# A convolution network's last two tiles, worked by halves of the images

## The chip, the cores and the metric

The kernel runs on one core of a Trainium2 chip, in one launch. A core has five engines that run beside each other: TensorE (PE, matmuls; its weight loads are listed as PEld), VectorE (DVE), ScalarE (ACT), GpSimd (POOL) and SyncE (SP, which here only issues DMAs). Sixteen DMA engines move data between the on-chip memory and DRAM. The metric is the time of the program on the device in microseconds; less is better. The span of a profile runs from the first to the last instruction of the profiled execution.

## The reference

The input is 1024 images of 16 x 16 pixels and 16 channels, in f32. Four layers follow each other, each of them `x = x + layer(norm(x))`, where the norm is taken over groups of channels. Layers 0 and 2 are a tensor-train product and a 3 x 3 convolution. Layers 1 and 3 are of one kind, and layer 3 is the one that the change touches:

```python
xt = jnp.transpose(x, (0, 3, 2, 1))
pre = _alive(xt)
y1 = _depthwise(xt, conv1_w, conv1_b)          # 3 x 3, per channel
y2 = _depthwise(xt, conv2_w, conv2_b)
p = jnp.concatenate([xt, y1, y2], axis=1)
flat = p.reshape(B * W * Hh, 48)
h = jax.nn.relu(flat @ fc0_w.T + fc0_b)        # 48 -> 128
d = (h @ fc1_w.T + fc1_b).reshape(B, C, W, Hh) # 128 -> 16
xn = xt + d
post = _alive(d)
xn = xn * (pre & post)
```

`flat` is cut into rows of 48 across the channel axis of an image, so one row of `fc0` mixes neighbouring pixels and channels of one image. All images are worked alike, and none depends on another.

## The kernel before, in words

**Tiles.** The images are worked in two chunks of 512 (`NB`). A chunk lies on chip as 32 tiles of 128 partitions by 512 columns: a column is an image, a partition one of 128 values, a tile is numbered `8 * q + w2`, with `q` a quarter of the channels and `w2` a pair of image columns. Two buffers, `X0` and `X1`, hold one chunk each. At the end of the kernel `layer_nca(X1, 1, 3, L3, xo)` works layer 3 on the second chunk in `X1`, while `output_steps(0)` writes the first chunk's images, which already lie in DRAM as tiles: it loads them line by line (`xs`), transposes them on VectorE (L1005) and stores them (L1010).

**Quads.** The work of `layer_nca` is a list of 64 quads `(q, w2, v)`. A quad is four rows of `fc0`, one in each of TensorE's four row groups. Each row is a sum of three small products, `T.matmul(ph, w, x)` at L1495, with 32 input rows, 128 outputs and 512 columns; the weights `wq` come from DRAM per quad. ScalarE applies bias and ReLU on the way out of PSUM (`hid`, L1498). Then `fc1` (L1346) brings the four hidden rows down to the outputs `po`; two quads, `v = 0` and `v = 1`, fill one tile.

**Order.** `plan()` writes the order of TensorE's work in advance, as slots: a slot is either one product in each row group or an `fc1`. It keeps a simple model of ScalarE (`evacs`, in slots), of six PSUM banks for `ph` (`BANKS`), and starts a quad at most two ahead of the `fc1` that is due. Work that follows is not waited for at once: `after(n, fn)` puts it n slots later. Each engine runs its own instructions strictly in the order of the program.

**The end of a tile.** `finish` adds bias and input into `u` on VectorE (L1358), `residual` multiplies by the mask and adds to the residual `r` (L1397, L1398), on GpSimd for all tiles but the last, (3, 7), which VectorE does. `fetch` has loaded `r` from DRAM when the tile's first `fc1` was emitted. On the second chunk `turn` follows eight slots later: four transposes on TensorE, one per 128 images (`ptx`, L1407; the PSUM pool `o` with its two banks is shared with `po`), and two copies on VectorE (`evac`, L159) into `xo`. `xo` is the buffer `X0` seen as `[image % 128, image group g, line h, column w, channel c]`, so that an image's values lie next to each other.

**The stores.** When all 32 tiles have been turned, eight DMAs of 1 MB store `xo` (L1657), two halves of the lines by four image groups. They stand behind the whole layer in the program.

**How `output_steps` is spread.** `run` takes steps with a lower and an upper bound as shares of the layer's slots, and interleaves them.

Of the kernel before, what the change touches and what calls it, by code (L numbers as in the profile page):

```python
# [12 lines left out]
ALU = mybir.AluOpType  # L13
# [5 lines left out]
B, S, C = 1024, 16, 16  # L19
P = 128  # L20
# [83 lines left out]
def conv_preact_kernel(ctx: ExitStack, tc: tile.TileContext, a: dict, out: bass.AP):  # L104
# [1180 lines left out]
    def layer_nca(X, n, l, L, xo=None):  # L1285


        st = {}
        quads = [(q, w2, v) for q in range(4) for w2 in range(8) for v in range(2)]
        AHEAD, FAR = 2, 3  # L1290
        BANKS, SKEW = 6, (0, 1, 2, 1)

        def rows_of(q, w2, v):
            return [16 * (4 * q + j) + 2 * w2 + v for j in range(4)]

        def weights(m):

            if m >= len(quads):
                return
            q, w2, v = quads[m]  # L1300
            slot = triple(2 * w2 + v)[1]
            if q > 0:
                st["wq", m] = work([P, 3, HID], "wq", "wq")
                nc.sync.dma_start(
                    st["wq", m],
                    L["wy"][q - 1].rearrange("g v h s k -> (g v h) s k")[:, slot : slot + 3],
                )

        def lines(m):


            if m >= len(quads) or triple(2 * quads[m][1] + quads[m][2])[0] < 2:
                return
            nx = st["nx", m] = work([P, 2, NB], "nx", "nx")
            for r in rows_of(*quads[m]):
                tiles = row_tiles(r)
                g = tiles[0][0] % 4
                over = [t[0] % C for t in tiles if t[0] % 4 != g]
                c, n1 = over[0], len(over)
                nc.sync.dma_start(  # L1320
                    nx[32 * g : 32 * g + 32, 0:n1],
                    X[32 * (c % 4) : 32 * (c % 4) + 32, 8 * (c // 4) : 8 * (c // 4) + n1],
                )
# [12 lines left out]
            for m in range(FAR):  # L1336
                lines(m)

        def fc1(q, w2, v, hid):
            if v == 0:  # L1340
                st["po"] = bank([P, NB], "o", "po1")
                if q > 0:
                    fetch(8 * q + w2)
            po = st["po"]
            for j in range(4):
                T.matmul(  # L1346
                    po[32 * j : 32 * j + 32], nca["w1"][:, v], hid[j], start=v == 0, stop=v == 1
                )
            if v == 1:
                finish(q, w2, po)  # L1350

        def finish(q, w2, po):
            if q == 0:
                V.tensor_scalar(
                    st["f", w2][64:96], po[96:128], nca["b1"][96:128], ALIVE, ALU.add, ALU.is_gt
                )
            u = st["u", q, w2] = work([P, NB], "u", "u")
            V.scalar_tensor_tensor(u, po, nca["b1"], X[:, 8 * q + w2], ALU.add, ALU.add)  # L1358
            if q > 0:
                residual(q, w2)  # L1360
                return

            ws = range(w2 - 1 if w2 else 0, 8 if w2 == 7 else w2)

            def masked():
                for w in ws:
                    mask(w)
                    residual(0, w)

            for w in ws:  # L1370
                fetch(w)
            after(3, masked)
# [17 lines left out]
            V.tensor_scalar(m, cnt[0], 0.5, None, ALU.is_gt)  # L1390
            V.scalar_tensor_tensor(m, cnt[1], 0.5, m, ALU.is_gt, ALU.mult)  # L1391

        def residual(q, w2):
            u, r = st["u", q, w2], st["r", q, w2]

            by = V if (q, w2) == (3, 7) else G
            by.tensor_tensor(u, u, st["m"][:, w2], ALU.mult)  # L1397
            by.tensor_tensor(r, r, u, ALU.add)  # L1398
            if xo is None:
                after(7, lambda: nc.sync.dma_start(tile_cw(xf[l + 1][n], 8 * q + w2), r))  # L1400
            else:
                after(8, lambda: turn(q, w2, r))

        def turn(q, w2, r):
            pt = psum([P, 4, 4, 2, S], "ptx")
            for bg in range(4):
                T.transpose(  # L1407
                    pt[:, bg].rearrange("p c v h -> p (c v h)"), r[:, bg * P : bg * P + P], ident
                )
            for v in range(2):  # L1410

                evac(
                    xo[:, :, :, 2 * w2 + v, 4 * q : 4 * q + 4].rearrange("p g h c -> p g c h"),
                    pt[:, :, :, v],
                )

# [7 lines left out]
        def plan():  # L1426

            todo = [[] for _ in range(4)]
            for m, quad in enumerate(quads):
                for j, r in enumerate(rows_of(*quad)):  # L1430
                    todo[row_tiles(r)[0][0] % 4].append((m, j, row_tiles(r)))
            left, ready = [4] * len(quads), [0.0] * len(quads)
            now, evacs, free_at, t, begun, f = [None] * 4, 0.0, [], 0, 0, 0
            while f < len(quads):
                if left[f] == 0 and ready[f] <= t:
                    yield f
                    f, t = f + 1, t + 1
                    continue
                free_at = [b for b in free_at if b > t]
                out = []  # L1440
                for g in range(4):
                    if now[g] is None and todo[g] and begun >= SKEW[g] and todo[g][0][0] <= f + 2:
                        if len(free_at) + sum(x is not None for x in now) < BANKS:
                            now[g] = [*todo[g].pop(0), 0]
                    if now[g] is not None:
                        m, j, tiles, k = now[g]
                        out.append((m, j, k))
                        now[g][3] += 1
                        if k == len(tiles) - 1:
                            evacs = max(evacs, t + 1.15) + 0.75  # L1450
                            free_at.append(evacs)
                            left[m], ready[m], now[g] = left[m] - 1, max(ready[m], evacs), None
                yield out
                t, begun = t + 1, begun + 1

        def step(slot):
            def go():
                t = st["slot"]
                if isinstance(slot, int):
                    q, w2, v = quads[slot]  # L1460
                    fc1(q, w2, v, [st["hid", slot, j] for j in range(4)])
                else:
                    for x in slot:
                        tile_of_row(*x)
                due = [fn for n, fn in later if n <= t]
                later[:] = [x for x in later if x[0] > t]
                for fn in due:
                    fn()
                st["slot"] = t + 1

            return go

        def tile_of_row(m, j, k):
            q, w2, v = quads[m]
            r = rows_of(q, w2, v)[j]
            tiles = row_tiles(r)
            if k == 0:
                if st.setdefault("begun", -1) < m:
                    st["begun"] = m
                    weights(m + AHEAD)  # L1480
                    lines(m + FAR)
                    if v == 0 and q == 0:
                        flags(w2)
                st["ph", m, j] = bank([P, NB], "h", "ph")
            ph = st["ph", m, j]
            ch, pair, pat = tiles[k]
            g = tiles[0][0] % 4
            rg = slice(32 * g, 32 * g + 32)
            if ch < C:
                w = nca["xw"][rg, XPATS.index(pat)]  # L1490
            else:
                w = st["wq", m][rg, TRIPLES[triple(2 * w2 + v)[0]].index(pat)]

            x = X[rg, 8 * (ch % C // 4) + pair] if ch % 4 == g else st["nx", m][rg, pair]
            T.matmul(ph, w, x, start=k == 0, stop=k == len(tiles) - 1)  # L1495
            if k == len(tiles) - 1:
                h = st["hid", m, j] = work([P, NB], "hid", "hid")
                A.activation(h, ph, AF.Relu, bias=nca["bt"][:, r : r + 1])  # L1498

        def rest():  # L1500
# [148 lines left out]
    with ExitStack() as es:  # L1649
        stage(es, dict(nca_sb, xs=2, xo=2), nca_ps)  # L1650

        xo = X0.rearrange("p n b -> p (n b)").rearrange("p (g h w c) -> p g h w c", g=4, h=S, w=S)
        run(layer_nca(X1, 1, 3, L3, xo), 280, (), (output_steps(0), 0.0, 1.0))
        for h in range(0, S, 8):
            for g in range(4):
                b0 = NB + g * P
                nc.sync.dma_start(  # L1657
                    out[b0 : b0 + P, h : h + 8].rearrange("b h w c -> b (h w c)"),
                    xo[:, g, h : h + 8].rearrange("p h w c -> p (h w c)"),
                )  # L1660


# [25 lines left out]
```

## Time and profile before

| | |
|---|---|
| Time, median of 3 runs | 3043.16 us (3041.85 to 3044.43) |
| Time of the profiled execution | 3042.73 us |
| Its span | 3041.0 us |
| Busy: PE / PEld / DVE / ACT / POOL | 98% / 41% / 58% / 36% / 22% |
| Mean DMA rate over the span | 138 GB/s |
| Rate while the image stores run | 376 GB/s |

The page's busy shares are means over all four layers. The tables by window show the busy time of each engine in a stretch (times are counted from the start of the span), then the granted clock of TensorE as a share of full speed, the busy share of the DMA engines and what they moved. In the chain of waits and in the timeline a line gives start, duration, engine, source line, the operation with its output and inputs, shapes, and the number of instructions merged. `xn` is the program's name for the buffers `X0` and `X1`, so a store `out_dram<-xn` reads `xo`. A f32 matmul leaves two records, and its end in the profile is modelled: what counts is the distance between starts.

### The profile page before, as it was taken

The numbers are of one execution on the slowest core, as the hardware profiler recorded it, in microseconds if no ns is written. First come the engines' busy times: TensorE is split into PE (matmuls) and PEld (weight loads), VectorE is DVE, ScalarE is ACT, GpSimd is POOL, SyncE is SP. The second block draws the span as 40 slices with busy tenths as digits, with TensorE's granted clock in tenths as the row PEclk, the third lists the DMA queues.
The fourth block names the chain that finished last, engine by engine and source line by source line (L and its number), as shares of the span: only waits on it lengthen the run. The fifth ranks groups of instructions, "written<-read, shape, count | busy, mean of one in ns | idle before, by whom it ended". The sixth has DMA issues, their size and how long they took to land.

```text
span 3041.0 us, 36525 instructions
## 1 busy us (share of the span) xinstructions
PE 2971.9 (98%) x13690; PEld 1239.6 (41%) x13690; DVE 1761.4 (58%) x2340; ACT 1099.3 (36%) x1806; POOL 671.6 (22%) x729
## 2 busy tenths in 40 slices
PE   7999999999999999999999999999999999999996
PEld 5544334444444444444444433333333333333332
DVE  5354337555554555544555668756977766856432
ACT  4431441000000000000101156666667656666563
POOL 1124670200000000000000015434542224432331
PEclk8999999999999999999999999999999999999998
DMA  8543664533334333332222235436437866343555
GB/s 310 225 126 99 147 150 151 166 109 109 109 109 149 124 109 109 109 102 88 88 88 94 71 131 167 137 119 204 124 121 183 193 109 199 123 127 110 155 158 197
DMA packets 251520, 418.37 MB, mean 138 GB/s; under 512 B 34868, under 2 KB 105064, under 8 KB 248272
## 3 DMA queue, kind: packets, MB, share of 16 engines
q1 hardware_dynamic: 225776, 362.53, 36.6%
q0 software_dynamic: 25376, 53.38, 8.5%
q8 instruction: 108, 1.77, 0.2%
q14 instruction: 68, 0.56, 0.1%
q10 hardware_dynamic: 192, 0.13, 0.0%
HBM read 238.58 MB, written 165.53 MB: 133 GB/s over the span
## 4 chain that ended last, share of the span: by engine, by line
PE 88%; issue 4%; POOL 2%; DVE 2%; DMA 2%; ACT 1%; SPq 0%; POOLq 0%; DVEq 0%; ACTq 0%
PE po L1134 51%; PE ph L1495 20%; PE po L1346 7%; PE pw L1057 3%; PE po L1222 2%; POOL xf L1271 1%; PE L_conv_pe L392 1%; PE ptin L866 1%; DVE bn L860 1%; POOL res L1398 1%; PE ptx L1407 1%; POOL u L1397 1%; PE po L1231 0%; ACT hx L1210 0%; DMA gq<-g_dram 0%
## 5 line engine op out<-in xcount | busy, mean ns | idle before, releaser
L1134 PE MATMUL po<-xn,w 128*128 128x512 f32 x3584 | 1575.6, 596 | 0.8 <-DVE xn L946 0.8
L1134 PEld LDWEIGHTS po<-xn,w 128*128 128x128 f32 x3584 | 670.8, 190 | 839.8 <-issue 820.9
L1498 ACT ACTIVATE hid<-ph,pack 128x512 f32<-128x512 f32 x1024 | 652.7, 686 | 381.5 <-PE ph L1495 271.6
L1170 DVE TENSOR_TENSOR r<-r,po 128x512 f32<-128x512 f32 x576 | 377.9, 684 | 577.5 <-PE po L1134 525.0
L1397 POOL TENSOR_TENSOR u<-u,mask 128x512 f32<-128x512 f32 x124 | 193.9, 1564 | 1820.9 <-DVE mask L1391 1404.2
L1062 ACT COPY w<-pw 128x512 f32<-128x512 f32 (+1 forms) x320 | 150.6, 557 | 1212.1 <-issue 1006.4
L1495 PE MATMUL ph<-xn,wq 32*128 32x512 f32 x3664 | 567.1, 611 | 0.0
L1495 PEld LDWEIGHTS ph<-xn,wq 32*128 32x128 f32 x3664 | 233.3, 184 | 270.0 <-issue 237.6
L1495 PE MATMUL ph<-xn,pack 32*128 32x512 f32 x1288 | 298.8, 625 | 4.9 <-ACT hid L1498 3.0
L1346 PE MATMUL po<-hid,pack 128*32 128x512 f32 x2048 | 281.7, 607 | 0.0
L1075 DVE TENSOR_TENSOR w<-w 128x512 f32<-128x512 f32 x320 | 210.9, 686 | 90.6 <-ACT w L1062 90.6
L655 DVE TENSOR_TENSOR xn<-xn,m 128x1024 f32<-128x1024 f32 x160 | 216.2, 1382 | 45.0 <-ACT m L678 44.8
L1358 DVE SCALAR_TENSOR_TENSOR u<-po,pack,xn 128x512 f32<-128x512 f32 x128 | 95.8, 749 | 203.3 <-PE po L1346 197.0
L1398 POOL TENSOR_TENSOR res<-res,u 128x512 f32<-128x512 f32 x124 | 206.5, 1666 | 9.7
L1222 PE MATMUL po<-xn,convw 128*128 128x512 f32 x368 | 166.2, 604 | 2.9 <-ACT conv L1270 2.9
L1495 PEld LDWEIGHTS ph<-xn,pack 32*128 32x128 f32 x1288 | 115.0, 185 | 104.3 <-issue 63.9
L1170 DVE TENSOR_TENSOR xn<-xn,po 128x512 f32<-128x512 f32 x96 | 64.4, 684 | 123.7 <-PE po L1134 123.3
L1346 PEld LDWEIGHTS po<-hid,pack 128*32 128x32 f32 x2048 | 42.8, 108 | 195.2 <-issue 144.3
L622 DVE TENSOR_TENSOR sq<-sq 128x1024 f32<-128x1024 f32 x78 | 109.8, 1407 | 13.3 <-ACT sq L640 12.6
L1222 PEld LDWEIGHTS po<-xn,convw 128*128 128x128 f32 x368 | 68.7, 191 | 99.7 <-issue 90.4
L404 POOL DMA_DIRECT2D L_conv_wy<-xn x160 | 88.8, 563 | 26.8 <-ACT xn L398 15.6
L1057 PE MATMUL pw<-R,gq 32*128 32x256 f32 (+1 forms) x1280 | 89.3, 384 | 2.9 <-DMA gq<-g_dram 2.8
(166 smaller groups left out, 1769.2 us busy)
## 6 DMA issues: line engine op xcount, KB each, us to landing
xf<-r SPq DMA_DIRECT2D x112, 512.0 KB, 3.8
xn<-xf SPq DMA_DIRECT2D x96, 512.0 KB, 4.9
r<-xf SPq DMA_DIRECT2D x80, 512.0 KB, 4.6
wq<-L_conv_wy SPq DMA_DIRECT2D x192, 192.0 KB, 2.8
res<-xf SPq DMA_DIRECT2D x128, 256.0 KB, 3.2
xf<-res SPq DMA_DIRECT2D x96, 256.0 KB, 2.1
res<-xr SPq DMA_DIRECT2D x256, 64.0 KB, 2.8
xf<-conv POOLq DMA_DIRECT2D x64, 256.0 KB, 5.7
```

Source lines behind the costliest of these rows:

```text
L655: V.tensor_tensor(part, part, m().unsqueeze(1).broadcast_to([P, 2, NB]), op)
L1057: T.matmul(pw[r][:, v], st["g", u][rows, v], st["R"][rows, p % 2, 64 * k0 : 256], start=True, stop=True,)
L1062: A.copy(w[:, k0:4, :, 32 * r : 32 * r + 32].rearrange("p k t (v o) -> p v (k t) o", v=2), pw[r],)
L1075: V.tensor_tensor(w[:, k], w[:, x], w[:, y], ALU.add if sign > 0 else ALU.subtract)
L1134: T.matmul(po, st["w", u][:, matrix, t], x, start=t == 0, stop=t == 3)
L1170: V.tensor_tensor(r[at], r[at], po, ALU.add if sign > 0 else ALU.subtract)
L1222: T.matmul(st["po", h][wh], conv["fw"][:, y], X[:, 16 * wh + h + y - 1], start=y == max(0, 1 - h), stop=y == min(2, S - h),)
L1346: T.matmul(po[32 * j : 32 * j + 32], nca["w1"][:, v], hid[j], start=v == 0, stop=v == 1)
L1397: by.tensor_tensor(u, u, st["m"][:, w2], ALU.mult)
L1398: by.tensor_tensor(r, r, u, ALU.add)
L1495: T.matmul(ph, w, x, start=k == 0, stop=k == len(tiles) - 1)
L1498: A.activation(h, ph, AF.Relu, bias=nca["bt"][:, r : r + 1])
```

## The change

The last four quads, those of the tiles (3, 6) and (3, 7), are each cut in two by images: first all four for images 0 to 255 of the chunk, then all four for images 256 to 511. A fourth member of a quad, `hf`, says which half it is; `None` is a whole quad. PSUM and work tiles are still allocated whole, and a half uses the first 256 columns of them. The second half uses the weights that the first half loaded, and the residual that it fetched. The mask and residual steps of these two tiles go to VectorE. `turn` makes two transposes for a half, and after tile (3, 7) of each half it issues the four stores of that half's two image groups. The eight stores at the end of the program go. `plan()` counts a half's evacuation as 1.9 slots and 1.0 instead of 1.15 and 0.75, and `output_steps` is spread over 0.93 of the layer.

```diff
-        quads = [(q, w2, v) for q in range(4) for w2 in range(8) for v in range(2)]
+        quads = [(q, w2, v, None) for q in range(4) for w2 in range(8) for v in range(2)]
+        if xo is not None:
+            quads[-4:] = [(3, w2, v, hf) for hf in range(2) for w2 in (6, 7) for v in range(2)]
+
+        def cols(hf):
+            return slice(0, NB) if hf is None else slice(hf * NB // 2, (hf + 1) * NB // 2)
+
+        def width(hf):
+            return slice(0, NB if hf is None else NB // 2)
...
             slot = triple(2 * w2 + v)[1]
-            if q > 0:
+            if hf == 1:
+                st["wq", m] = st["wq", m - 4]
+            elif q > 0:
                 st["wq", m] = work([P, 3, HID], "wq", "wq")
...
             if v == 0:
-                st["po"] = bank([P, NB], "o", "po1")
-                if q > 0:
+                st["po"] = bank([P, NB], "o", "po1")[:, width(hf)]
+                if q > 0 and hf != 1:
                     fetch(8 * q + w2)
...
-            u = st["u", q, w2] = work([P, NB], "u", "u")
-            V.scalar_tensor_tensor(u, po, nca["b1"], X[:, 8 * q + w2], ALU.add, ALU.add)
+            u = st["u", q, w2] = work([P, NB], "u", "u")[:, width(hf)]
+            V.scalar_tensor_tensor(u, po, nca["b1"], X[:, 8 * q + w2, cols(hf)], ALU.add, ALU.add)
...
-            by = V if (q, w2) == (3, 7) else G
-            by.tensor_tensor(u, u, st["m"][:, w2], ALU.mult)
+            by = V if (q, w2) == (3, 7) or hf is not None else G
+            by.tensor_tensor(u, u, st["m"][:, w2, cols(hf)], ALU.mult)
             by.tensor_tensor(r, r, u, ALU.add)
...
-        def turn(q, w2, r):
-            pt = psum([P, 4, 4, 2, S], "ptx")
-            for bg in range(4):
+        def turn(q, w2, r, hf):
+            g0, n = (0, 4) if hf is None else (2 * hf, 2)
+            pt = psum([P, 4, 4, 2, S], "ptx")[:, 0:n]
+            for bg in range(n):
...
+            if (q, w2) == (3, 7):
+                for h in range(0, S, 8):
+                    for g in range(g0, g0 + n):
+                        b0 = NB + g * P
+                        nc.sync.dma_start(
+                            out[b0 : b0 + P, h : h + 8].rearrange("b h w c -> b (h w c)"),
+                            xo[:, g, h : h + 8].rearrange("p h w c -> p (h w c)"),
+                        )
...
-                            evacs = max(evacs, t + 1.15) + 0.75
+                            evacs = max(evacs, t + (1.15 if quads[m][3] is None else 1.9))
+                            evacs += 0.75 if quads[m][3] is None else 1.0
...
-                st["ph", m, j] = bank([P, NB], "h", "ph")
+                st["ph", m, j] = bank([P, NB], "h", "ph")[:, width(hf)]
...
+            x = x[:, cols(hf)]
             T.matmul(ph, w, x, start=k == 0, stop=k == len(tiles) - 1)
             if k == len(tiles) - 1:
-                h = st["hid", m, j] = work([P, NB], "hid", "hid")
+                h = st["hid", m, j] = work([P, NB], "hid", "hid")[:, width(hf)]
...
-        run(layer_nca(X1, 1, 3, L3, xo), 280, (), (output_steps(0), 0.0, 1.0))
-        for h in range(0, S, 8):
-            for g in range(4):
-                b0 = NB + g * P
-                nc.sync.dma_start(
-                    out[b0 : b0 + P, h : h + 8].rearrange("b h w c -> b (h w c)"),
-                    xo[:, g, h : h + 8].rearrange("p h w c -> p (h w c)"),
-                )
+        run(layer_nca(X1, 1, 3, L3, xo), 280, (), (output_steps(0), 0.0, 0.93))
```

More of the change, by code (lines that the diff above doesn't have):

```diff
@@ L1299, in weights @@
                 return
-            q, w2, v = quads[m]
+            q, w2, v, hf = quads[m]
             slot = triple(2 * w2 + v)[1]
-            if q > 0:
+            if hf == 1:
+                st["wq", m] = st["wq", m - 4]
+            elif q > 0:
                 st["wq", m] = work([P, 3, HID], "wq", "wq")
@@ L1314, in lines @@
             nx = st["nx", m] = work([P, 2, NB], "nx", "nx")
-            for r in rows_of(*quads[m]):
+            for r in rows_of(*quads[m][:3]):
                 tiles = row_tiles(r)
@@ L1337, in start, with fc1 @@
                 lines(m)
-        def fc1(q, w2, v, hid):
+        def fc1(q, w2, v, hf, hid):
             if v == 0:
-                st["po"] = bank([P, NB], "o", "po1")
-                if q > 0:
+                st["po"] = bank([P, NB], "o", "po1")[:, width(hf)]
+                if q > 0 and hf != 1:
                     fetch(8 * q + w2)
@@ L1349, in fc1, with finish @@
             if v == 1:
-                finish(q, w2, po)
-        def finish(q, w2, po):
+                finish(q, w2, hf, po)
+        def finish(q, w2, hf, po):
             if q == 0:
@@ L1356, in finish @@
                 )
-            u = st["u", q, w2] = work([P, NB], "u", "u")
-            V.scalar_tensor_tensor(u, po, nca["b1"], X[:, 8 * q + w2], ALU.add, ALU.add)
+            u = st["u", q, w2] = work([P, NB], "u", "u")[:, width(hf)]
+            V.scalar_tensor_tensor(u, po, nca["b1"], X[:, 8 * q + w2, cols(hf)], ALU.add, ALU.add)
             if q > 0:
-                residual(q, w2)
+                residual(q, w2, hf)
                 return
@@ L1391, in mask, with residual @@
             V.scalar_tensor_tensor(m, cnt[1], 0.5, m, ALU.is_gt, ALU.mult)
-        def residual(q, w2):
-            u, r = st["u", q, w2], st["r", q, w2]
-            by = V if (q, w2) == (3, 7) else G
-            by.tensor_tensor(u, u, st["m"][:, w2], ALU.mult)
+        def residual(q, w2, hf=None):
+            u, r = st["u", q, w2], st["r", q, w2][:, cols(hf)]
+            by = V if (q, w2) == (3, 7) or hf is not None else G
+            by.tensor_tensor(u, u, st["m"][:, w2, cols(hf)], ALU.mult)
             by.tensor_tensor(r, r, u, ALU.add)
@@ L1401, in residual @@
             else:
-                after(8, lambda: turn(q, w2, r))
-        def turn(q, w2, r):
-            pt = psum([P, 4, 4, 2, S], "ptx")
-            for bg in range(4):
+                after(8, lambda: turn(q, w2, r, hf))
+        def turn(q, w2, r, hf):
+            g0, n = (0, 4) if hf is None else (2 * hf, 2)
+            pt = psum([P, 4, 4, 2, S], "ptx")[:, 0:n]
+            for bg in range(n):
                 T.transpose(
@@ L1412, in turn @@
                 evac(
-                    xo[:, :, :, 2 * w2 + v, 4 * q : 4 * q + 4].rearrange("p g h c -> p g c h"),
+                    xo[:, g0 : g0 + n, :, 2 * w2 + v, 4 * q : 4 * q + 4].rearrange(
+                        "p g h c -> p g c h"
+                    ),
                     pt[:, :, :, v],
                 )
+            if (q, w2) == (3, 7):
[6 more added lines that the diff above has]
+                        )
         later = []
@@ L1429, in plan @@
             for m, quad in enumerate(quads):
-                for j, r in enumerate(rows_of(*quad)):
+                for j, r in enumerate(rows_of(*quad[:3])):
                     todo[row_tiles(r)[0][0] % 4].append((m, j, row_tiles(r)))
@@ L1459, in go @@
                 if isinstance(slot, int):
-                    q, w2, v = quads[slot]
-                    fc1(q, w2, v, [st["hid", slot, j] for j in range(4)])
+                    q, w2, v, hf = quads[slot]
+                    fc1(q, w2, v, hf, [st["hid", slot, j] for j in range(4)])
                 else:
@@ L1473, in tile_of_row @@
         def tile_of_row(m, j, k):
-            q, w2, v = quads[m]
+            q, w2, v, hf = quads[m]
             r = rows_of(q, w2, v)[j]
```

## The prediction

> **What bounds the kernel now.** I read the page's rows first (PE busy in 98% of the span, so for most of it only TensorE work counts), then the chain of waits from 2950 us on, the table of windows over the last 51 us, and the timeline. Only the end of the span concerns this change. The table of windows (PE, PEld, DVE, ACT, POOL busy, granted clock, DMA share, GB/s) cuts it in two:
>
> ```profile
> 2990.00:3000.00 10.00, 10.00 (x88) 3.71 (x80) 1.86 (x4) 6.24 (x10) 2.42 (x2) 1.00 0.53 170
> 3000.00:3010.00 10.00, 10.00 (x68) 3.75 (x66) 5.39 (x10) 6.63 (x11) 3.60 (x3) 1.00 0.15 52
> 3010.00:3018.66 8.66, 5.71 (x27) 1.70 (x26) 4.09 (x7) 0.83 (x2) 1.27 (x1) 0.90 0.00 0
> 3018.66:3041.00 22.34, 0.00 (x0) 0.00 (x0) 0.00 (x0) 0.00 (x0) 0.00 (x0) 0.50 0.91 376
> ```
>
> Until 3010 TensorE is never idle and the DMA engines have room; for the last 22.34 us no engine computes at all, and the DMA share is 0.91. These 22.34 us are the eight image stores, which the chain and the timeline show starting only after the last tile's chain on TensorE and VectorE:
>
> ```profile
> 3012.32 1.90 PE po L1346 x8
> ...
> 3014.32 0.76 DVE u L1358
> ...
> 3015.10 0.70 DVE u L1397
> ...
> 3015.83 0.70 DVE res L1398
> ...
> 3016.67 0.93 PE ptx L1407 x4
> ...
> 3017.62 0.58 DVE xn L159
> 3018.20 0.43 DVEq L1684
> ```
> ```profile
> 3018.66 8.23 SPq L1657 DMA_DIRECT2D out_dram<-xn  x8
> ```
> ```profile
> DMA to landing us min/median/max: 3.9/10.2/14.4
> ```
>
> The first store lands 3.9 us after 3018.66, at 3022.6; the last, issued at 3025.6, lands 14.4 later, at 3040.0. So each further 1 MB takes (3040.0 - 3022.6)/7 = 2.49 us, 421 GB/s, and 0.95 us of closing waits follow. Eight stores cost 3.9 + 7 x 2.49 + 0.95 = 22.3 us from the first issue, four stores 12.3. What can be hidden is at most the difference, 10 us; what is hidden depends on when the first store can be issued, because all eight queue on the same saturated engines.
>
> For the price of TensorE work, three rows of the timeline (one whole quad, then the next fc1) and three of another stage, where the same kind of matmul (32 rows, four row groups) is 256 wide:
>
> ```profile
> 2994.78 1.06 PE L1346 MATMUL po<-hid,pack 128*32 128x512 f32 x8
> ...
> 2995.78 2.86 PE L1495 MATMUL ph<-xn,wq 32*128 32x512 f32 x24
> ...
> 2998.56 1.07 PE L1346 MATMUL po<-hid,pack 128*32 128x512 f32 x8
> ```
> ```profile
> 1710.28 0.74 PEld L1057 LDWEIGHTS pw<-R,gq 32*128 32x128 f32 x16 [0.76 <-issue]
> 1710.28 1.15 PE L1057 MATMUL pw<-R,gq 32*128 32x256 f32 x16
> ...
> 1711.36 0.70 PE L1134 MATMUL po<-xn,w 128*128 128x512 f32 x1
> ```
>
> Four matmuls run side by side and each f32 product is two records, so 24 records are six rounds and 8 are two. A full fc1 takes 1.00 us (2994.78 to 2995.78), three full slots 2.78; with 0.43 us a round the eight rounds are 3.43 and changing the kind of matmul costs the other 0.35 (some 0.22 of it with the ph group, 0.14 with fc1). The 256-wide example is four rounds in 1.08 us (1710.28 to 1711.36): 4 x 0.215 + 0.22. Half the width is half the round, the fixed part stays.
>
> **The change part by part.** (1) Four quads of 512 columns become eight of 256, in the order 6, 7 of the first half, 6, 7 of the second. Streaming time is the same; fixed time is paid four more times, 4 x 0.35 = 1.4 us, and the plan written by hand over these quads has 261 slots instead of 241, four of them fc1 and the others thinner tile slots.
>
> (2) When the first store can go. I counted the plan's order after the diff from the fc1 of (3,4,1), at 2990.41 in the trace and untouched, up to `turn(3, 7)` of the first half, which falls due 8 slots after its fc1, behind slot 253. On TensorE lie: 3 full fc1 at 1.00 = 3.0; 5 half fc1 at 1.00 - 2 x 0.215 = 0.57, together 2.85 (one of them already of the second half); 3 full transposes at 0.59 (chain row of ptx x4) and one half at 0.37, 2.14; 8 groups of tile slots with 0.22 fixed, 1.76; 4 slots with a full tile at 0.86 = 3.43; 23 half slots at 0.43 = 9.89 (one more, slot 224, runs in other row groups beside the full tile of slot 223 and costs nothing). Sum 23.1 us; the joints are counted slightly twice, since the same sum over the old order comes out some 0.3 too late against the trace, so I take 22.8: the last transposes start at 3013.2. From there to the first store it was 1.99 us before (3016.67 to 3018.66); with two transposes fewer and copies of half width I take 1.8. **First stores at 3015.0 instead of 3018.66.** ScalarE is not on this path: a 256-wide evacuation should cost 0.69 less 0.21 (128x256 against 128x512 copies of L1062: 0.387 and 0.600), and each fc1 has at least 0.3 us to spare; were a half evacuation as dear as a full one, the store would move by 0.2.
>
> (3) VectorE takes over the mask and the residual of (3,6), from GpSimd, and runs them in halves. No row has these at 256 columns. Bounds: 0.69 each (no gain from half the width) and 0.35 (no fixed part); I take 0.43, the 512 row less 256 elements at its own rate. At 0.69 the stores come 0.3 us later. VectorE is busy 5.39 of 10 us there; its `output_steps` transposes end ahead of these copies. The turn of (3,5) still waits for GpSimd, 3.3 us after its fc1 (u at 2999.84, end 3003.2 before); eight slots, now mostly half slots, are some 4.5 us, so it just fits. If that cover goes, TensorE stalls for the rest, at most 1 us.
>
> (4) Second half: fc1 of (3,6,1) at 3013.8, two more fc1, three half slots and 0.22: last fc1 done about 3017.6, then u, mask, residual (1.4), transposes, copies and issue (1.8): stores at 3020.3. That is 1.7 later than before, but only four stores follow: 3020.3 + 12.3 = 3032.6. The queue ends later: 3015.0 + 22.3 = **3037.4**. So the DMA engines set the end, the second half's stores wait behind the first's, and the delayed end of compute costs nothing.
>
> (5) On SP, four stores stand behind slot 253; nothing is queued behind them but the other four, since the second half has no `wq` loads and no `fetch`. The `wq` loads stay as many: the second half keeps the tiles of the first. `output_steps` ends at 0.93 of 262 slots (slot 244) instead of 1.0 of 242: the last line's store goes ahead of the image stores in SP's order, where else it would wait behind slot 261. It is 512 KB at a DMA share of 0.15, so nothing. The eight stores' sizes and issue times stay.
>
> Sum: 3018.66 - 3015.0 = 3.6 us off the span of 3041.0. The profiled execution took 3042.73, 1.73 around its span, and the median is 0.43 above it; I predict 3043.16 - 3.6, **3039.5 us**, 0.12% less.
>
> **A rule against the change.** In the 256-wide rows weight loads fill 0.74 of the four rounds, 0.185 a round, and still the rounds start 0.215 apart. The Trainium skill, "TensorE: Matmul & The Clock Gate", section "Part 3: Packing small matmuls", says that a weight load overlaps running matmuls only where the row group differs (another section allows a background buffer). Here all four groups are in use in every round, so by the rule a half round costs 0.215 + 0.185 = 0.40. Some 46 half rounds lie in front of the first store, with the fc1 left aside: 8.5 us more. The sum would be 3023.5 for the first store, and an end at 3045.8 of span. At 512 columns one cannot tell the readings apart, but the trace's 256-wide rows decide: I take 0.215.
>
> **The rivals.**
> A. *Weight loads become the bound (slower).* The rule above, in place: tile slots 224 to 253. It decides from a round of about 0.295 us: (0.295 - 0.215) x 46 = 3.7 eats the whole gain. At 0.40 the time is about 3048. For it: with 0.185 of 0.215 filled there is little room, and the ph tiles change weights in every round. Against it: four consecutive rounds of just this shape. Chance 0.05.
> B. *The second half's copies into `xo` wait for the first half's stores to land.* Four stores from 3015.0 have landed at 3026.4; copies and issue 2, then 12.3: 3040.8, no change, 3043. For it: both are one tile, X0. Against it: the image groups are the outermost axis of `xo`, so the ranges are disjoint. Chance 0.06.
> C. *Stalls in the new order* (the turn of (3,5), a bank of `o`, a late evacuation): 1 to 3 us of gain lost, 3041 to 3042. The order puts more slots between things that now take half the time. Chance 0.12.
> D. *The first half's stores really hide*: the end is set by the second half, 3032.6, a gain of 8.4 and 3034.8. It needs the first stores before about 3010, and TensorE's order puts 22.8 us in front of them; nothing in the profile lets that shrink by 5. Chance 0.05.
> The forecast itself, limited by the DMA queue from an earlier start, gain 2.3 to 5: 0.72.
>
> **How the numbers follow.** The forecast's own range is 3038.2 to 3040.9. For 8 in 10 I add C and half of the repeat spread of the medians (3041.85 to 3044.43 for three runs): 3037.5 to 3042.0. About 0.2%, 6.1 us, is what a measurement of this kernel can tell from no change: faster by more needs D, or a gain far above my count (0.10); slower by more needs A and a stall of C on top of it (0.03); the rest is within (0.87).
>
> **What would show it.** In the changed kernel's timeline: two groups of four image stores, the first issued near 3015, the second near 3020.3; eight landings 2.5 us apart without a gap; an end 22.3 us after the first issue. ph rounds of 32x256 start 0.215 apart, ptx groups of two transposes. A first store after 3018.7, or rounds of 0.3 us and more, means A; a second group issued after 3026, B; an idle gap between fourth and fifth landing means that the queue did not set the end. The forecast is wrong if the first store leaves before 3012.

## The result, and the profile after

The changed kernel takes 3039.69 us in the median of 20 runs (3035.54 to 3043.34), the kernel before 3044.4 us in as many (3040.77 to 3048.66): a ratio of 0.9985, with a 95% interval of 0.9980 to 0.9991. That is 4.7 us less, between 2.7 and 6.1. The profiled execution took 3039.35 us with a span of 3037.6.

Single runs of either kernel spread over some 8 us, more than the change is worth. The traces show spread ahead of the tail: `u` of the tile (3,3) starts at 2984.55 in the trace after, and at 2985.89 to 2987.59 in those of experiments 1, 3 and 10, whose code up to there is the same. Behind it they agree: the first store of all four comes 23.8 us after the fc1 of (3,4,1). So in what follows all times named **T** count from that fc1, which stands 6.90 us behind the start of `u` of (3,3) in both kernels. From the timeline before, and after:

```profile
2983.51 0.75 DVE L1358 SCALAR_TENSOR_TENSOR u<-po,pack,xn 128x512 f32<-128x512 f32 x1 [6.45 <-PE po L1346]
...
2990.41 1.07 PE L1346 MATMUL po<-hid,pack 128*32 128x512 f32 x8
```
```profile
2984.55 0.75 DVE L1370 SCALAR_TENSOR_TENSOR u<-po,pack,xn 128x512 f32<-128x512 f32 x1 [6.44 <-PE po L1358]
...
2991.45 1.07 PE L1358 MATMUL po<-hid,pack 128*32 128x512 f32 x8
```

Where that fc1 was itself shifted (three tiles by halves), the 6.90 are kept. The end is then at T = 50.6 before and 46.2 after, 4.4 us less.

The table of windows of the changed kernel (columns as before: PE, PEld, DVE, ACT, POOL busy, granted clock, DMA share, GB/s):

```profile
2990.00:3000.00 10.00, 10.00 (x96) 4.74 (x88) 2.28 (x5) 5.62 (x11) 2.43 (x2) 1.00 0.80 220
3000.00:3010.00 10.00, 10.00 (x130) 6.46 (x126) 5.87 (x13) 6.65 (x16) 2.45 (x2) 1.00 0.15 54
3010.00:3015.60 5.60, 5.60 (x70) 3.58 (x63) 2.64 (x8) 3.72 (x10) 0.00 (x0) 1.00 0.00 0
3015.60:3020.50 4.90, 3.07 (x25) 1.50 (x23) 3.46 (x10) 1.25 (x4) 0.00 (x0) 1.00 0.91 375
3020.50:3037.60 17.10, 0.00 (x0) 0.00 (x0) 0.00 (x1) 0.00 (x0) 0.00 (x0) 0.54 0.92 383
```

The DMA share is 0.91 from 3015.6 on, while TensorE still works on the second half, and 0.92 in the stretch without compute, which has shrunk from 22.3 us to 17.1. The chain of waits still runs through TensorE and VectorE to the second half's last copy:

```profile
3014.22 0.37 PE ptx L1420 x2
...
3016.64 1.26 PE po L1358 x16
...
3019.47 0.42 PE ptx L1420 x2
...
3019.92 0.37 DVE xn L159
3020.29 0.21 DVEq L1704
```

But this chain no longer sets the end. The view of the line of the stores (duration of an issue, first and last issue, then the time to landing, that is, until the transfer is complete):

```profile
L1435 SPq DMA_DIRECT2D out_dram<-xn x8: 332/1084/1268, 3015.3 to 3023.5; - x8
...
DMA to landing us min/median/max: 3.9/9.1/13.1
```

The first store is issued at 3015.27 and lands after 3.9 us; the last is issued at 3023.53 and lands 13.1 later, at 3036.66. Seven intervals in 17.5 us are 2.50 us each, as before the change, and in the trace no interval between landings is longer than 2.53, also not between the fourth and the fifth store, which were issued 3.4 us apart. From the first issue to the end it is 22.3 us, as before.

And the price of the halves on TensorE, from the timeline (its matmul rows, and the weight loads of one group, PEld):

```profile
2995.82 1.07 PE L1358 MATMUL po<-hid,pack 128*32 128x512 f32 x8
2996.81 2.00 PE L1521 MATMUL ph<-xn,wq 32*128 32x256 f32 x24
...
3000.32 1.34 PEld L1521 LDWEIGHTS ph<-xn,wq 32*128 32x128 f32 x24 [0.84 <-issue]
3000.32 1.74 PE L1521 MATMUL ph<-xn,wq 32*128 32x256 f32 x24
...
3001.99 0.64 PE L1358 MATMUL po<-hid,pack 128*32 128x256 f32 x8
...
3002.56 1.74 PE L1521 MATMUL ph<-xn,wq 32*128 32x256 f32 x18
3004.23 0.66 PE L1420 MATMUL ptx<-ident,res 128*128 128x128 f32 x4
3004.82 0.64 PE L1358 MATMUL po<-hid,pack 128*32 128x256 f32 x8
```

A half fc1 takes 0.57 us (3001.99 to 3002.56), as expected. A group of tile slots takes 1.67 us (3000.32 to 3001.99, and 3002.56 to 3004.23), whether it holds three full slots (24 records) or four thin ones (18 records).

### The profile page after: what moved, and what is told of

Read it like the earlier page. It is cut to its first block, busy times and chain, and to the rows that moved or that the text cites. A ratio compares the mean times of both kernels' runs of the same rounds, so it can differ in the third digit from the quotient of the medians.

```text
span 3037.6 us, 36802 instructions
## 1 busy us (share of the span) xinstructions
PE 2973.1 (98%) x13810; PEld 1245.4 (41%) x13810; DVE 1764.0 (58%) x2352; ACT 1102.7 (36%) x1822; POOL 669.9 (22%) x727
## 4 chain that ended last, share of the span: by engine, by line
PE 92%; DVE 2%; DMA 1%; issue 1%; ACT 1%; POOL 1%; SPq 0%; DVEq 0%; POOLq 0%; ACTq 0%
PE po L1134 51%; PE ph L1521 22%; PE po L1358 8%; PE po L1222 4%; PE pw L1057 3%; PE po L1231 1%; PE L_conv_pe L392 1%; PE ptin L866 1%; DVE bn L860 1%; PE ptx L1420 1%; PE pvar L753 1%; PE pr L765 0%; PE pmean L749 0%; POOL res L1410 0%; ACT hx L1210 0%
## 5 line engine op out<-in xcount | busy, mean ns | idle before, releaser
L1524 ACT ACTIVATE hid<-ph,pack 128x512 f32<-128x512 f32 (+1 forms) x1040 | 656.2, 680 | 381.3 <-PE ph L1521 267.7
L1521 PE MATMUL ph<-xn,wq 32*128 32x512 f32 (+1 forms) x3752 | 568.8, 600 | 0.0
L1521 PEld LDWEIGHTS ph<-xn,wq 32*128 32x128 f32 x3752 | 239.4, 184 | 268.2 <-issue 235.9
L1358 PE MATMUL po<-hid,pack 128*32 128x512 f32 (+1 forms) x2080 | 282.1, 602 | 0.0
L1370 DVE SCALAR_TENSOR_TENSOR u<-po,pack,xn 128x512 f32<-128x512 f32 (+1 forms) x130 | 96.3, 741 | 189.9 <-PE po L1358 185.6
L622 DVE TENSOR_TENSOR sq<-sq 128x1024 f32<-128x1024 f32 x78 | 109.8, 1408 | 13.3 <-ACT sq L640 12.6
```

What stands on the lines that cost most here:

```text
L1358: T.matmul(po[32 * j : 32 * j + 32], nca["w1"][:, v], hid[j], start=v == 0, stop=v == 1)
```

## The experiments

**1. Stores behind the last tile.** The halves stay; the stores of both are issued where the second half's were.

```diff
-            if (q, w2) == (3, 7):
+            if (q, w2) == (3, 7) and hf == 1:
                 for h in range(0, S, 8):
-                    for g in range(g0, g0 + n):
+                    for g in range(4):
```

> The halves stay, but all eight stores are issued after the last tile of the second half. Times are counted from the fc1 of (3,4,1) to the end of the span: 50.6 us in the kernel before (2990.41 to 3041.0), 46.1 in the changed one (2991.45 to 3037.6). Theory (the gain is the earlier start of the store queue, the halving itself only costs): the last tile is ready at 29.1 instead of 28.2, so the whole is 29.1 + 22.3 = 51.4, about 0.8 us slower than the kernel before. Rival (working by halves shortens the tail by itself): it keeps part of the gain, 47 to 50.

Measured: 3040.01 us, ratio 0.9982 (0.9976 to 0.9989), first store at T = 23.8, end at T = 46.5. Neither reading foresaw this, and the fault was in the edit: it moved the stores in the program, but did not take the early start away. The order of the loop is image groups 0 and 1 first, they depend on the first half's copies alone, and nothing else stood in SP's queue. Two stores went out at 3018.30 and 3018.70 while the second half was worked, and the third at 3023.57. The table of windows shows it:

```profile
3008.30:3018.30 10.00, 10.00 (x129) 6.42 (x126) 4.43 (x12) 6.72 (x17) 0.00 (x0) 1.00 0.11 38
3018.30:3023.57 5.27, 3.40 (x26) 1.79 (x26) 3.75 (x10) 1.59 (x4) 0.00 (x0) 1.00 0.86 358
3023.57:3040.90 17.33, 0.00 (x0) 0.00 (x0) 0.00 (x0) 0.00 (x0) 0.00 (x0) 0.54 0.91 375
```

Two stores in flight nearly bridge the gap: the second lands at 3024.68 and the third 2.8 us later. What released a store here is the data it reads and its place in SP's own queue, not its place among the other engines' instructions. It also disposes of rival B: the third store, of image group 2, is issued before the second, of group 1, has landed, so the copies into the groups 2 and 3 didn't wait for it.

**2. The second half's stores first.** The same, with `for g in (2, 3, 0, 1)` outermost, so that the head of SP's queue needs the second half.

> As the first experiment, with the eight stores behind the last tile, but those of the second half's images first, so that nothing in SP's order can go while the second half is worked (there, two stores of the first half went at 23.8 us after the fc1 of (3,4,1), because only the data held them). Theory: first store at 29.1, end 29.1 + 22.3 = 51.4 from that fc1, 5.2 us later than the changed kernel and 0.8 later than the kernel before. Rival (halving shortens the tail by itself): 46 to 50.

Measured: 3046.47 us, ratio 1.0006 (0.9998 to 1.0014), first store at T = 29.1, end at T = 51.4.

```profile
3014.40:3024.39 9.99, 8.12 (x86) 4.78 (x80) 5.70 (x15) 4.75 (x12) 0.00 (x0) 1.00 0.00 0
3024.39:3046.70 22.31, 0.00 (x0) 0.00 (x0) 0.00 (x0) 0.00 (x0) 0.00 (x0) 0.52 0.91 376
```

The 22.31 us without compute are back. So halving alone costs 0.8 us (51.4 against 50.6), and the whole gain, 5.2 us against this run, is the earlier start of the queue.

**3. One store less.** The store of group 1, second half of the lines, is left out.

> One of the first half's four 1 MB stores is left out (that part of the output is not written). Theory (all eight stores are one saturated queue from the first issue on): the end comes one store, 2.5 us, earlier, 43.6 from the fc1 of (3,4,1). Rival (the first half's stores are hidden behind the second half, and the second half's four set the end): the same end as the changed kernel, 46.1.

Measured: end at T = 43.7, 2.5 us before the changed kernel; 3037.32 us. The line of the stores:

```profile
L1437 SPq DMA_DIRECT2D out_dram<-xn x7: 332/906/1262, 3016.6 to 3024.9; - x7
...
DMA to landing us min/median/max: 3.9/8.0/10.6
```

A store of the *first* half, issued while compute goes on, costs its full 2.5 us at the end: the queue is the bound from its first store on.

**4. The turn after 4 slots.** `after(8 if hf is None else 4, ...)` in `residual`.

> A half's turn is due 4 slots after its fc1 instead of 8. Counted from the fc1 of (3,4,1). Theory (the end is the first store plus 22.3): the residual of (3,7), first half, is ready at 20.5 and its turn now stands behind the next fc1, at 21.0 instead of 22.7, so the first store goes at 22.1 instead of 23.8 and the end comes at 44.4, 1.7 us before the changed kernel's and 6.1 before the kernel before. Rival (the second half sets the end, or the earlier transposes stall TensorE for the residual): 46 or more, as the changed kernel.

Measured: first store at T = 22.1, end at T = 44.5; 3039.34 us, ratio 0.9981 (0.9972 to 0.9989). To 0.1 us what was expected. Against the changed kernel's ratio of 0.9985 the intervals overlap; only the traces resolve these 1.7 us.

**5. Three tiles by halves.** `w2 in (5, 6, 7)`, `st["wq", m - 6]`, six `wq` buffers.

> The last three tiles are worked by halves instead of the last two (six weight buffers instead of five). From the fc1 of (3,4,1); a full tile takes 8.15 us of TensorE, a half one 4.85. Theory (first store plus 22.3, until the second half's last store plus 12.3 is later): the first store goes 8.15 - 4.85 = 3.3 earlier, at 20.5, the second half's 1.55 later, at 30.6; the ends would be 42.8 and 42.9, so about 43, 3.2 us before the changed kernel. Rival (the halved work costs more than its cover): the end is 46 or later.

Measured: first store at T = 20.5, second half's at 30.6, both as expected, but the end at T = 44.6 instead of 43; 3037.95 us, ratio 0.9981 (0.9973 to 0.9989). In the trace the third store lands 4.3 us behind the second (3017.84 and 3022.14) instead of 2.5, and what was lost is never caught up. The DMA view of the stretch has one transfer that the changed kernel's has not:

```profile
q8 instruction: 1, 0.02, 0.2%
```

It is 16 KB on one engine at 3019.12 and takes 0.89 us; four 8 KB packets around it, between 3017.3 and 3020, took 435 to 713 ns instead of 315, 0.95 more in all. Together these are the 1.8 us, if they lay on one engine, and the last four packets of the run are alone in the trace, 0.3 us apart, when all others are done. So it looks as if one of 16 engines had run late and each landing waited for it. Over all traces the two go together: such a transfer fell among the image stores in the five runs of experiments 5, 6, 7, 11 and 12, and all five have a landing some 1.8 us late; in the others it came before the first store, and none has. But no run took the transfer away; the cause fits the numbers and is not shown.

**6. Three tiles and 4 slots,** then **7. also with `output_steps` over 0.87.**

> Three tiles by halves, and a half's turn due after 4 slots instead of 8. From the fc1 of (3,4,1), an estimate from the runs with three tiles (first store 20.5, second half's 30.6, end 44.6) and with 4 slots (1.7 earlier): first store 18.8, second half's stores at 30.6 at the latest. Theory: the end is the later of 18.8 + 22.3 = 41.1 and 30.6 + 12.3 = 42.9, so 42.9: compute of the second half now sets it and the queue runs empty ahead of the fifth store. Rival (the 1.8 us that the third landing lost in the run with three tiles is a cost of halving three tiles): 44.6 again, with the same late landing.

Measured: first store at T = 18.6, second half's at 30.6, end at T = 44.2; 3038.32 us, ratio 0.9978 (0.9968 to 0.9988). The last 0.5 MB store of `output_steps` was issued at 3014.11, between the first half's four and the second's, and the late third landing came again. So the fifth store had to queue: it landed 5.1 us after its issue, where a first store takes 3.9.

> As three tiles by halves with the turn after 4 slots, and output_steps spread over 0.87 of the layer, so that its last 0.5 MB store no longer falls between the first half's four. From the fc1 of (3,4,1), as in the runs with three tiles: first store 18.6, second half's stores from 30.6. Theory: four stores have landed at 30.0 before the fifth is issued, the second half's compute sets the end, 30.6 + 12.3 = 42.9, against 44.2 with the 0.5 MB store in between and 46.1 in the changed kernel. Rival (a 16 KB instruction transfer on one DMA engine, which came at 3019 in both runs with three tiles, holds all later landings back): 44.2 or more.

Measured: first store at T = 18.6, end at T = 43.1; 3036.98 us, ratio 0.9975 (0.9965 to 0.9985). The windows:

```profile
3000.00:3010.63 10.63, 10.63 (x142) 6.94 (x142) 4.46 (x12) 7.67 (x18) 0.00 (x0) 1.00 0.18 52
3010.63:3022.53 11.90, 9.60 (x110) 5.41 (x106) 5.80 (x15) 6.08 (x14) 0.00 (x0) 0.98 0.86 352
3022.53:3035.12 12.59, 0.00 (x0) 0.00 (x0) 0.00 (x0) 0.00 (x0) 0.00 (x0) 0.50 0.81 334
```

Now the stretch without compute is 12.6 us, four stores, and the second half's compute sets the end: the late landing of the third store came here too, and cost nothing: the fifth, issued at 3022.53, landed 3.9 us later, as a first store does, although the fourth had landed only at 3023.86. This version has the lowest median of all that were tried, 7.2 us below the kernel before it in the same runs.

**8. `output_steps` over the whole layer.** 1.0 for 0.93.

> output_steps spread over the whole layer again (1.0 instead of 0.93). Its last transposes then stand behind slot 246 and its last store behind slot 261, in SP's order behind the first half's four stores and before the second half's. Theory: VectorE takes 2.3 us for these transposes between the residual of (3,7), first half, and its copies, which still have 0.5 us to spare or lose up to 1, and the queue carries 0.5 MB more in the tail, 1.25 us: end at 47.4 to 48.4 from the fc1 of (3,4,1), 1.2 to 2.2 more than the changed kernel. Rival (0.93 was of no use): 46.1.

Measured: first store at T = 23.8, end at T = 47.8; 3043.01 us, ratio 0.9993 (0.9985 to 1.0001). VectorE's transposes delayed nothing. The 0.5 MB store came last of all, behind the eighth image store in SP's queue, and landed 1.5 us after it:

```profile
3019.53 9.52 SPq L1435 DMA_DIRECT2D out_dram<-xn  x8
3029.09 1.26 SPq L1010 DMA_DIRECT2D out_dram<-xo  x1
```

It cost 1.6 us. Without this small part of the change, over a third of the gain by the traces is gone.

**9. The plan's old numbers.** 1.15 and 0.75 for halves too.

> plan() counts a half's evacuation as a whole one's, 1.15 and 0.75 slots, instead of 1.9 and 1.0. The order then has 259 slots instead of 261 and puts each fc1 up to one slot closer behind its last evacuation. Theory (TensorE is the bound and ScalarE has some 0.3 us to spare at the tightest fc1): TensorE waits for ScalarE by 0.1 to 0.3 us at three or four fc1, the first store goes 0 to 1 us later than 23.8 from the fc1 of (3,4,1). Rival (the plan's numbers decide the gain): 2 us and more later.

Measured: first store at T = 25.2, end at T = 47.5; 3041.97 us, ratio 0.999 (0.9981 to 0.9998). 1.3 us later, between the two readings: two of the fc1 of halves take 0.78 and 0.66 us instead of 0.57, and the groups behind them grow to 30 and 26 records and 2.8 and 2.7 us. Which wait carries it was not taken apart.

**10. Mask and residual on GpSimd.** `by = V if (q, w2) == (3, 7) else G`.

> Mask and residual of the tile (3,6) stay on GpSimd for both halves. Theory: the residual is ready some 0.8 us later, but its turn comes 3.5 us after the fc1 on TensorE anyway, so the first store stays at 23.8 from the fc1 of (3,4,1) and the end at 46.1. Rival (VectorE's taking over these steps was needed): the turn waits and the first store goes 0.5 us or more later.

Measured, in one execution: first store at T = 23.8, end at T = 46.2. As the changed kernel; moving these steps to VectorE brings nothing here.

**11. Four parts,** and **12. four parts, the tile (3,5) on VectorE too.** 128 images each; the edits are those of the change with 4 for 2 (`range(4)`, `NB // 4`, one image group), and in the second `by = V if (q, w2) >= (3, 5) else G`.

> The last two tiles in four parts of 128 images. If weight loads and products overlap and the slower of the two sets a round (0.185 for the loads against 0.108 for 128 columns), rounds of ph start 0.185 to 0.19 apart, a group of tile slots takes about 1.5 us, the last stores are issued some 43 us after the fc1 of (3,4,1) and the end is near 50, later than in the changed kernel (46.1). If loads never set the pace, rounds are 0.108, the group 1.0, and the end 43. If they were added to the products, the rounds would be 0.29.

> As four parts, with mask and residual of the tiles (3,5) to (3,7) all on VectorE. With four parts TensorE stood still for 1.2 us before the turn of (3,5), for GpSimd's residual, and its granted clock went to 0.50 soon after and stayed there for some 16 us; before that the rounds of 128 columns came 0.11 apart. Theory (loads of weights overlap products and never set the pace; the clock fell with the stall): no stall, clock 1.00 to the last tile, rounds of 0.11, the end near 44 from the fc1 of (3,4,1). Rival (narrow rounds alone lower the clock): the clock is 0.50 again for a good part and the end is near 50.

Measured, in one execution each: ends at T = 52.4 and 46.8. In the first, TensorE stood 1.0 us for GpSimd's residual of (3,5), and its granted clock fell to 0.50 soon after, for 17 us. In the second this wait is gone, but TensorE stood 0.9 us for a copy of VectorE's, and the clock stayed at 1.00. Timeline and windows of the first:

```profile
3004.82 0.70 PE L1420 MATMUL ptx<-ident,res 128*128 128x128 f32 x4 [0.97 <-POOL res L1410]
...
3011.03 1.73 PE L1521 MATMUL ph<-xn,wq 32*128 32x128 f32 x24
3012.69 0.66 PE L1358 MATMUL po<-hid,pack 128*32 128x128 f32 x8
```
```profile
3003.00:3006.00 3.00, 2.03 (x30) 1.28 (x22) 1.79 (x4) 0.87 (x4) 1.69 (x2) 0.88 0.30 99
3006.00:3009.00 3.00, 3.00 (x46) 2.35 (x44) 1.35 (x5) 1.99 (x7) 0.00 (x0) 0.50 1.02 264
...
3018.00:3021.00 3.00, 3.00 (x42) 2.01 (x35) 1.68 (x5) 1.29 (x6) 0.00 (x0) 0.50 1.03 418
```

and of the second, the standstill and a group of the same size:

```profile
3007.33 0.43 PE L1358 MATMUL po<-hid,pack 128*32 128x128 f32 x8 [0.89 <-DVE xn L159]
...
3012.68 1.22 PE L1521 MATMUL ph<-xn,wq 32*128 32x128 f32 x24
3013.82 0.42 PE L1358 MATMUL po<-hid,pack 128*32 128x128 f32 x8
```
```profile
3006.00:3009.00 3.00, 2.12 (x41) 1.57 (x37) 1.94 (x6) 1.74 (x6) 0.00 (x0) 1.00 0.48 154
...
3015.00:3018.00 3.00, 3.00 (x65) 2.24 (x59) 2.19 (x8) 2.24 (x8) 0.00 (x0) 1.00 1.02 410
```

So the standstill alone does not explain the fall of the clock: one of nearly the same length in the same work left it at 1.00, and so did one of 1.2 us in the changed kernel (from 3018.26, clock 1.00 until 3021.75, when TensorE had done). The rival of narrow rounds alone is refuted by the second run; what lowered the clock in the first stays open.

At full clock the rounds of 128 columns start 0.11 us apart in the trace (a group in 1.14), at the granted clock of 0.50 they start 0.21 apart (a group in 1.66). So a round follows the columns down to 128; a weight load, 0.185 us long, sets no floor at 0.185, and in the trace loads of successive rounds overlap too (starts at 3012.78, 3012.89 and 3013.01).

The second run's end is 2.8 us later than expected, by its DMA queue. Two 0.5 MB stores of `output_steps`, at 3014.00 and 3021.60, fell between the image stores, as in experiment 6: an estimate of 2.5 us at the rate of the others. The first store at T = 19.9, the 22.3 of eight stores and these 2.5 make 44.7. The missing 2.1 are like the late landing of experiment 5, and the DMA view of the stretch has two such transfers:

```profile
q8 instruction: 2, 0.03, 0.4%
```

## Why the prediction was right

**The mechanism and the time.** 3039.5 us were predicted, 3039.69 measured; but part of this closeness is luck. The prediction took 3.6 us off a median of 3043.16. The gain was 4.4 by the traces and 4.7 by the medians, off a kernel before that came out at 3044.4 with more runs. The size was a fifth too small, and most of that is one term of step (2).

**Step (2), the first store.** Predicted for T = 24.6, measured at 23.8.
- Nearly all of the error, 0.7 of 0.8 us, is in one term. From the last transposes to the first store 1.8 us were taken, and 1.12 measured (3014.15 to 3015.27). The 1.99 us before were taken as the model, but there the transposes stood behind a wait and mostly at half the clock (0.55 in the row below), and both copies moved twice the data; two copies of 128 columns end 0.62 us after the first begins.

```profile
3016.67:3018.66 1.99, 0.91 (x4) 0.51 (x4) 1.81 (x4) 0.00 (x0) 0.00 (x0) 0.55 0.00 0
```

- The tile slots were counted as one slot after the other, 15.1 us, less 0.3 for the joints. Measured: 2.79 + 1.93 + 6 x 1.67 = 14.7. The sum agrees and its parts don't, which is luck. A group's fixed part is 0.37 (1.67 less six rounds of 0.216) rather than 0.22: in the trace of the group at 3000.32 one row group ends some 0.18 behind the others. But a group of four thin slots costs no fourth slot (1.67 and not 1.94), as no row group has more than six rounds in it. A slot is a matter of the plan; on the engine the row groups run on by themselves.

**Step (3).** A mask or residual step of 256 columns takes 0.42 to 0.43 us; 0.43 was taken. The turn of (3,5) "just fits" was right, with little to spare: GpSimd ends at 3003.96 and the transposes start at 3004.23. Experiment 11 is what happens when this cover goes: a stall of 1.0 us, as the prediction said ("at most 1 us").

**Step (1) and step (4), the end.** The second half's stores were predicted for T = 29.9 and came at 29.1; the difference is again the 1.8 us. (The 3017.6 in that step does not fit its own terms, which give 3017.0; the 3020.3 does.) They came 0.8 us later than the stores before, not 1.7. By the chains TensorE's last fc1 ended 2.6 us later than before (T = 26.4 and 23.8), more than the 1.4 of fixed time in step (1), and the half-wide steps behind it won 1.8 back. The end came 22.3 us after the first store, as predicted. Experiments 3 and 4 show that this is the rule here, and experiment 7 where it stops.

**Step (5).** The last store of `output_steps` was put at "nothing", rightly for 0.93. It was said that it would otherwise stand behind slot 261; experiment 8 gives this its price, 1.6 us.

**The rivals.** A, weight loads as the bound, and the rule of the Trainium skill behind it ("TensorE: Matmul & The Clock Gate", Part 3) are refuted at this shape: rounds of 256 columns start 0.216 apart in the changed kernel, and of 128 columns 0.11 apart (experiment 12), in groups that load all four row groups. B is refuted by experiment 1, and in the changed kernel itself the second half's store is issued at 3020.53 while the second of the first half lands only at 3021.66. C left no trace in the changed kernel: TensorE has no gap ahead of the first store. D did not happen with two tiles; with three, an earlier turn and `output_steps` over 0.87 the second half did set the end (experiment 7).

## What to carry to other kernels

When a kernel ends in a stretch where only stores run, find out from landings and DMA share whether they are one saturated queue; then the end is the first issue plus the sum of all transfers, and the only thing that counts is how early the first may go, until the second part's own compute takes over. Work the last pieces so that one part of the output is complete early, look in the queue for any other transfer that falls into the tail, and let the delay before the issue be as short as the data allows. Where a change is worth less than the spread of single runs, count traces from a common event just ahead of it.

## What the runs showed of the hardware that was not expected

- In one run the granted clock of TensorE fell to 0.50 within 2 us of the start of a standstill of 1.0 us, and stayed there for 17 us although matmuls came without a pause. A standstill of 0.9 us in nearly the same work, and one of 1.2 us in the changed kernel, did not bring it down as fast. The cause is open.
- Weight loads of 0.185 us did not keep rounds of four matmuls from following each other at 0.11 us.
- In all three runs with three tiles by halves, and in both with four parts, a landing came some 1.8 us late, in a stretch with an instruction transfer of 16 KB, while the bytes moved at the usual rate. That one late engine held the landings back is likely and not shown.
- Single runs of one kernel differ by some 8 us, 0.26%, while the tails of traces with the same work there agree to 0.1 us (first store at T = 23.8 in the changed kernel and in experiments 1, 3, 8 and 10).
